# Two graph layers on one core: the q and k projections taken for two pairs of batch elements at once, with a new written order of work

## The chip, the core and the metric

The kernel runs on one core of one Trainium2 chip. The metric is the device time in microseconds of one execution of the whole kernel, from the inputs in HBM to the output in HBM. For the kernel before the change it is the median of three runs. One further execution was taken by the hardware profiler; the views below come from it.

## The reference

128 batch elements of 128 nodes with 512 features go through two layers; all values are float32. The first layer is masked attention with 8 heads of 64 features, the second a graph attention whose scores are sums of two numbers per node. Each has a residual and a normalisation without weights.

```python
# x: (128, 128, 512), adj: (128, 128) of 0 and 1
q = (x @ Wq + bq).reshape(b, n, H, HD)      # H = 8, HD = 64; k and v alike
scores = einsum('bqhd,bkhd->bhqk', q, k) / sqrt(HD) + (1 - adj) * -1e9
attn = softmax(scores)
x = layernorm(x + einsum('bhqk,bkhd->bqhd', attn, v).reshape(b, n, d) @ Wo + bo)

h = x @ W;  s1 = h @ a1;  s2 = h @ a2
e = leaky_relu(s1[:, :, None] + s2[:, None, :], 0.2) * adj
x = layernorm(x + elu(softmax(e) @ h + beta * h))
```

## The kernel before

The batch is worked off in 64 pairs `g` of two elements `b0` and `b1`. A pair is needed because the five products with a 512 x 512 weight (`q`, `k`, `v`, `w` for Wo, `h` for the second layer's W) are each done by seven block products instead of eight: the weight is cut into 2 x 2 blocks of 256 x 256, and x into two halves of its features for each of the two elements. `weight_sum` prepares the sums of weight blocks once. `block_sum` (L245) makes four sums of x blocks per pair on GpSimd, and the seven calls `product(name, g, n)` (L278) with n = 1 to 7 accumulate in PSUM, in `main` (n = 1, 2, 3, 5, 6) and `side` (n = 7, 4). `take_part` (L344) copies a partial sum out to SBUF, on ScalarE for q, k, v and h, on VectorE for w, and `add_block` (L360, VectorE) adds a further part to what was copied. So an accumulator is read while it is still going to grow, and the next product into it waits for that read.

For v, w and h the x side is the stationary operand and the weight streams past it, 256 columns in one matmul. For q and k it is the other way round, because their output has to have features in partitions: a weight block of 128 x 128 is stationary and x streams past it, one element's 128 nodes, so 128 columns in one matmul. A float32 matmul of the source appears in the trace as two matmul instructions. A product of q or k is thus 8 instructions of 128 columns, a product of v, w or h 4 instructions of 256 columns.

The rest of a pair's way, by function: `turn_x` (L237) transposes x blocks on VectorE after `fetch_blocks` has loaded them; `scores` (L370) and `mask`, `row_max`, `exps`, `normalise` make the attention weights; `attn_write` (L422) stores them in a DRAM scratch and `attn_read` (L427) fetches them back with rows and columns of blocks exchanged, as four DMAs; `turn_attn` (L444, VectorE) finishes the transposition; `attend` (L454) multiplies with v. Then come `w`, a normalisation (`norm_c`), the second layer's edge weights, which also take a way through DRAM, `aggregate` (L642), `h` and the final normalisation (`norm_f`) and `store`. `fetch_x` loads x once more for the residual.

Nothing is scheduled by the compiler. Each function call is given a place, in microseconds, by `at(place, fn, ...)`; the calls are sorted by place and issued in that order, each on its own engine's queue, and semaphores keep the data dependencies. The places are the result of a planner that was run beforehand with a cost for each call; only their order reaches the chip. `rows(g)` gives the places of a pair relative to `g * STEP`, with `STEP = 36.678`; `other` replaces them for the first and last pairs, and `last_rows` holds the order of the last two. Several pairs are under way at once: q and k of a pair are multiplied in the step before its scores, h about 2.5 steps after them. The places of the way through DRAM, for example, are these:

```python
            (12.283, exps, b1, 0), (12.823, attn_write, b0), (16.179, exps, b1, 1),
...
            (21.248, normalise, b1, 3), (21.546, attn_read, b0), (21.948, turn_attn, b0, 0),
            (22.433, attn_write, b1), (23.511, take_part, "v", g, 5, 1, 1),
            (24.964, product, "v", g, 3), (26.507, turn_attn, b0, 1),
            (27.155, add_block, "v", g, 7, 1, 1), (27.181, attn_read, b1),
            (30.486, product, "v", g, 4), (31.193, take_part, "v", g, 3, 0, 1),
            (31.929, turn_attn, b1, 0), (32.334, turn_attn, b1, 1),
            (32.982, add_block, "v", g, 4, 1, 0), (36.883, attend, b1), (38.699, attend, b0),
```

Nearly all DMAs are issued by SyncE (SP), in order; a DMA whose data or buffer isn't ready holds up those behind it. Before the first product, `keep_busy(15, "early")` runs 15 matmuls on an identity (L136). At the end, the last pair does w and h by plain products (`plain`, `end_product`, L671), in halves of 256 columns for h, and `end_store` (L710) writes halves of rows.

## Time and profile before

| | before |
|---|---|
| median of 3 runs | 2378.44 us (2378.03 to 2378.46) |
| profiled execution, its own time | 2378.15 us |
| its span, first to last instruction | 2376.4 us |
| mean granted TensorE clock | 0.998 |
| busy: TensorE / VectorE / ScalarE / GpSimd | 99% / 83% / 67% / 36% of the span |
| DMA | 269.83 MB, mean 114 GB/s |

The span is about 1.8 us shorter than the execution's time. "Busy" counts overlapping matmuls once. In the profile PE is TensorE's matmul side and PEld its weight loads, DVE is VectorE, ACT is ScalarE, POOL is GpSimd, and a "q" behind an engine's name is its queue of DMA issues. PEclk is the TensorE clock that was granted, as a share of full speed.

### The profile page before, as it was taken

The page shows a single profiled execution, that of the slowest core. Times are in us where ns is not written, and L with a number is a line of the kernel's source. Part 1 is how long each engine was busy: PE and PEld are TensorE (multiplying, and loading weights), DVE is VectorE, ACT ScalarE, POOL GpSimd, SP SyncE. Part 2 cuts the span into 40 slices and gives each one's busy share as a digit, 9 for nine tenths or more (in the row PEclk, how much of TensorE's full clock was granted, in tenths as well). Part 3 has the DMA queues.
Part 4 walks back from the last instruction along what each step waited for, and adds up shares of the span by engine and source line. Part 5 has one row for each costly group of instructions (what it writes and reads, how often), then busy time and mean ns, then how long its engine had stood idle before and what let it go on. Part 6 is the DMA issues. An engine that isn't in the chain of part 4 may idle for free.

```text
span 2376.4 us, 50868 instructions
## 1 busy us (share of the span) xinstructions
PE 2354.4 (99%) x17703; PEld 2177.5 (92%) x17703; DVE 1961.7 (83%) x4390; ACT 1591.1 (67%) x5763; POOL 865.5 (36%) x1044
## 2 busy tenths in 40 slices
PE   8999999999999999999999999999999999999998
PEld 8998999999999999999999999999999999999996
DVE  7788788888888888888888888888888888888887
ACT  4675666766766667667666676676666766766665
POOL 6243333433433333334334333343343333433422
PEclk9999999999999999999999999999999999999999
DMA  6333334334343343343443433424434334344432
GB/s 192 108 100 112 116 101 125 107 105 134 92 120 119 107 118 108 108 128 92 121 122 103 119 108 111 126 92 121 123 103 119 107 112 125 92 120 122 116 115 74
DMA packets 256121, 269.83 MB, mean 114 GB/s; under 512 B 57372, under 2 KB 204840, under 8 KB 255480
## 3 DMA queue, kind: packets, MB, share of 16 engines
q1 hardware_dynamic: 254992, 265.45, 37.8%
q8 instruction: 140, 2.29, 0.4%
q14 instruction: 117, 0.96, 0.1%
q0 software_dynamic: 304, 0.85, 0.1%
q10 hardware_dynamic: 568, 0.27, 0.0%
HBM read 157.62 MB, written 108.85 MB: 112 GB/s over the span
## 4 chain that ended last, share of the span: by engine, by line
PE 96%; DMA 1%; DVE 1%; ACT 1%; issue 0%; SPq 0%; POOLq 0%; POOL 0%; DVEq 0%; ACTq 0%
PE pq L307 12%; PE pk L307 12%; PE pv L301 12%; PE ph L301 11%; PE pw L301 11%; PE eq L307 9%; PE psc L379 5%; PE po L454 5%; PE pz L642 5%; PE eh L301 5%; PE ew L301 4%; PE ev L301 4%; DMA xblk<-in_x_dram 1%; DMA wq_sb<-in_L_gnn_Wq_dram 0%; ACT s L401 0%
## 5 line engine op out<-in xcount | busy, mean ns | idle before, releaser
L435 POOL TENSOR_TENSOR x<-x,bo_b_in 128x512 f32<-128x512 f32 x128 | 163.6, 1279 | 863.3 <-DMA x<-in_x_dram 863.3
L401 ACT ACTIVATE s<-s,nmax 128x128 f32<-128x128 f32 x1024 | 396.9, 396 | 61.4 <-DVE nmax L395 61.3
L415 ACT ACTIVATE sb<-s,rinv 128x128 f32<-128x128 f32 x1024 | 325.3, 392 | 0.0
L355 ACT ACTIVATE kT<-pk,bias_c 128x128 f32<-128x128 f32 x512 | 160.2, 364 | 202.2 <-PE pk L307 143.2
L355 ACT ACTIVATE qT<-pq,bias_c 128x128 f32<-128x128 f32 x512 | 160.6, 368 | 157.6 <-PE pq L307 157.6
L505 DVE SCALAR_TENSOR_TENSOR ya<-w,wa_row 128x512 f32<-128x512 f32 x256 | 223.9, 875 | 4.4
L401 ACT ACTIVATION_READ_ACCUMULATOR s<-s,nmax 128x1 f32 x1024 | 199.2, 195 | 0.0
L466 ACT ACTIVATE oT<-po,bias_c 128x128 f32<-128x128 f32 x512 | 139.5, 382 | 80.5 <-PE po L454 80.5
L352 DVE TENSOR_TENSOR w<-pw,x 128x256 f32<-128x256 f32 x252 | 106.3, 422 | 97.3 <-PE pw L301 90.8
L444 DVE STREAM_TRANSPOSE attnT<-ab 128x512 f32<-128x512 f32 x256 | 172.7, 694 | 6.8 <-DMA ab<-scr 6.6
L387 DVE SCALAR_TENSOR_TENSOR s<-psc,amask 128x512 f32<-128x512 f32 x256 | 168.6, 680 | 0.7 <-PE psc L379 0.7
L395 DVE TENSOR_REDUCE nmax<-s 128x8 f32<-128x1024 f32 x128 | 156.1, 1220 | 4.3
L349 ACT COPY h<-ph 128x256 f32<-128x256 f32 x252 | 93.8, 372 | 94.1 <-PE ph L301 94.0
L349 ACT COPY v<-pv 128x256 f32<-128x256 f32 x256 | 94.6, 369 | 84.4 <-PE pv L301 59.9
L240 DVE STREAM_TRANSPOSE xT<-xblk 128x512 f32<-128x512 f32 x128 | 139.4, 1108 | 7.9 <-DMA xblk<-in_x_dram 7.9
L657 DVE SCALAR_TENSOR_TENSOR u<-h,x 128x512 f32<-128x512 f32 x126 | 87.1, 692 | 63.8 <-ACT h L349 61.6
L260 POOL TENSOR_TENSOR tx<-xT 128x256 f32<-128x256 f32 x128 | 94.7, 741 | 119.8 <-PE psc L379 97.1
L301 PE MATMUL pv<-wv_sb,xT 128*128 128x256 f32 x512 | 137.5, 392 | 0.0
L307 PE MATMUL pq<-xT,wq_sb 128*128 128x128 f32 x1024 | 135.9, 276 | 1.2 <-DMA wq_sb<-in_L_gnn_Wq_dram 1.2
L307 PE MATMUL pk<-xT,wk_sb 128*128 128x128 f32 x1024 | 134.8, 275 | 0.6 <-DMA wk_sb<-in_L_gnn_Wk_dram 0.4
L307 PEld LDWEIGHTS pq<-xT,wq_sb 128*128 128x128 f32 x1024 | 130.1, 193 | 4.5 <-issue 1.3
L307 PEld LDWEIGHTS pk<-xT,wk_sb 128*128 128x128 f32 x1024 | 129.1, 192 | 4.2 <-DMA wk_sb<-in_L_gnn_Wk_dram 0.6
(677 smaller groups left out, 6352.6 us busy)
## 6 DMA issues: line engine op xcount, KB each, us to landing
scr<-sb SPq DMA_DIRECT2D x128, 512.0 KB
ab<-scr SPq DMA_DIRECT2D x512, 128.0 KB
x<-in_x_dram SPq DMA_DIRECT2D x128, 256.0 KB
xblk<-in_x_dram SPq DMA_DIRECT2D x254, 128.0 KB
out_dram<-u SPq DMA_DIRECT2D x126, 256.0 KB
pb<-s2d SPq DMA_DIRECT2D x62, 128.0 KB
attd<-att SPq DMA_DIRECT2D x62, 128.0 KB
ab<-attd SPq DMA_DIRECT2D x248, 32.0 KB
```

Source lines behind the costliest of these rows:

```text
L301: nc.tensor.matmul(out, b[:, c, :], a[:, c, :], start=first and c == 0, stop=(c == 1), skip_group_check=True,)
L307: nc.tensor.matmul(out[:, m * N : (m + 1) * N], a[:, c, m * P : (m + 1) * P], b[:, c, :], start=first and m == 0 and c == 0, stop=(c == 1) ...
L349: nc.scalar.copy(dst, src)
L355: nc.scalar.activation(dst[:, m, :], src[:, m * N : (m + 1) * N], AF.Identity, bias=BIAS[name][:, 2 * i + m : 2 * i + m + 1],)
L387: nc.vector.scalar_tensor_tensor(s_t[b][:, j * HP : (j + 1) * HP, :], psc[b][j], SCALE, amask.rearrange("p (o n) -> p o n", o=1).broadcast ...
L395: nc.vector.tensor_reduce(nmax[b], s_t[b], AX.X, ALU.max, negate=True)
L401: nc.scalar.activation(s_t[b][:, h, :], s_t[b][:, h, :], AF.Exp, bias=nmax[b][:, h : h + 1], accum_out=rsum[b][:, h : h + 1],)
L415: nc.scalar.mul(sb[b][:, :, h, :], s_t[b][:, h, :].rearrange("p (b c) -> p b c", c=Q), rinv[b][:, h : h + 1],)
L435: nc.gpsimd.tensor_tensor(xr[b], xr[b], later["bo"], ALU.add)
L444: nc.vector.transpose(attnT[b].rearrange("p h (a r) -> p a h r", r=Q)[:, rows], ab[b].rearrange("p a (h c) -> p a h c", c=Q)[:, rows],)
L466: nc.scalar.activation(oT[b][:, c, :], src[:, c, :], AF.Identity, bias=bv_c[:, c : c + 1])
L505: nc.vector.scalar_tensor_tensor(z, y[b], 1.0, wa_row[j], ALU.mult, ALU.mult, accum_out=s12[g][:, i, j : j + 1])
```

## The change

q and k are multiplied once for two pairs. The transposed x of an even and of the following odd pair lie side by side in one tile, `xT_all`, and their block sums in `xs_all`, so that `factor` gives q and k a moving operand of 256 columns; v still takes one pair's 128 as its stationary operand. `product` for q and k is called for even `g` only; its matmuls are half as many and twice as wide. Each of q and k now has three PSUM tiles of its own, for n = 1, for n = 2 and for n = 7, where a pair before had one each and one shared. `take_part` and `add_block` for q and k move twice as many columns per instruction, and `scores` picks its pair out of the common tile. v's SBUF buffers go from two to four; those of xT and its block sums from two to one for each of the two pairs.

The places are new throughout: `STEP = 72.624` is the step of two pairs, and `rows` has a list for even pairs (with q and k) and one for odd pairs (without). The whole order of the first and last pairs is new too. At the start, x blocks of pairs 0 and 1 are loaded first, half by SP's queue and half by ScalarE's; the small loads on GpSimd's queue (`adj`, `bo`, `a1`, `beta`) move behind the first block sums; the matmuls on the identity go from 15 to 20. At the end the last element's row is stored whole, and the other's halves by two queues.

The diff, without most of the lists of numbers:

```diff
--- before.py
+++ after.py
@@ -16,7 +16,7 @@
 EPS = 1e-5
 ALPHA = 0.2
 NEG = 1000000000.0
-STEP = 36.678
+STEP = 72.624
...
     def load_blocks(g):
-        t = grp.tile([P, G, 4, P], F32, tag="xb", name=f"xblk_{g}", bufs=1)
+        if g == 1:
+
+            t = wk2.tile([P, H, N], F32, tag="attnT", name="xblk_1")
+            t = t.rearrange("p (t b) d -> p t b d", t=G)
+        else:
+            t = grp.tile([P, G, 4, P], F32, tag="xb", name=f"xblk_{g}", bufs=1)
         for a in range(4):
-            (nc.scalar if g == 0 and a >= 2 else nc.sync).dma_start(
+            (nc.scalar if g < 2 and a >= 2 else nc.sync).dma_start(
                 out=t[a * Q : (a + 1) * Q].rearrange("r t b d -> r (t b) d"),
                 in_=x[g * G : (g + 1) * G, :, a * P : (a + 1) * P].rearrange(
                     "t (b r) d -> r (t b) d", r=Q
...
-    xblk, xn = {0: load_blocks(0)}, {}
+    xblk, xn = {0: load_blocks(0), 1: load_blocks(1)}, {}
...
-    early = keep_busy(15, "early")
+    early = keep_busy(20, "early")
...
     later = {}
 
     def load_later():
+        nc.gpsimd.dma_start(out=adj_sb, in_=adj)
         later["beta"] = broadcast(cpool, beta, 1, "beta_b")
+        later["bo"] = broadcast(cpool, bo, D, "bo_b")
         for j in range(2):
             a_j = a1[j * D : (j + 1) * D].rearrange("f o -> (f o)")
             later["a", j] = broadcast(wk2, a_j, D, "uf")
-        later["bo"] = broadcast(cpool, bo, D, "bo_b")
 
...
-    xT, right, tx, qT, kT, vb, y, hp, main, side, oT, zT, xr = ({} for _ in range(13))
+    right, tx, qT, kT, vb, y, hp, main, side, oT, zT, xr = ({} for _ in range(12))
     BIAS = {"q": bq_c, "k": bk_c}
     OUT = {"q": qT, "k": kT, "v": vb, "w": y, "h": hp}
 
+
+
+    xT_all = cpool.tile([P, NC, G, 2, N], F32, tag="xT", name="xT")
+    xs_all = cpool.tile([P, 4, 2, 2, N], F32, tag="tx", name="tx")
+
     def turn_x(g, t):
-        if t == 0:
-            xT[g] = grp.tile([P, NC, G * N], F32, tag="xT", name=f"xT_{g}")
         nc.vector.transpose(
-            xT[g][:, :, t * N : (t + 1) * N].rearrange("p m (b r) -> p b m r", r=Q),
+            xT_all[:, :, t, g % 2, :].rearrange("p m (b r) -> p b m r", r=Q),
             xblk[g][:, t].rearrange("p b (c m) -> p b m c", c=Q),
         )
 
+    def x_blocks(slots):
+        s = slice(slots, slots + 1) if isinstance(slots, int) else slice(0, 2)
+        b = [xT_all[:, 2 * h : 2 * h + 2, j, s] for h in range(2) for j in range(G)]
+        t = [xs_all[:, i, :, s] for i in range(4)]
+        b11, b12, b21, b22, t1, t2, t3, t4 = (a.rearrange("p c s n -> p c (s n)") for a in b + t)
+        return b11, b12, b21, b22, (t1, t2, t3, t4)
+
     def block_sum(name, g, n):
 
         if name == "x":
-            b11, b12 = xT[g][:, :2, :N], xT[g][:, :2, N:]
-            b21, b22 = xT[g][:, 2:, :N], xT[g][:, 2:, N:]
+            b11, b12, b21, b22, (t1, t2, t3, t4) = x_blocks(g % 2)
         else:
             src = oT if name == "w" else zT
             b11, b12 = src[g * G][:, :2], src[g * G + 1][:, :2]
             b21, b22 = src[g * G][:, 2:], src[g * G + 1][:, 2:]
-        if (name, g) not in tx:
-            tx[name, g] = grp.tile(
-                [P, 4, 2, N], F32, tag=f"t{name}", name=f"t{name}_{g}", bufs=2 if name == "x" else 1
-            )
-        t1, t2, t3, t4 = (tx[name, g][:, i] for i in range(4))
+            if (name, g) not in tx:
+                tx[name, g] = grp.tile(
+                    [P, 4, 2, N], F32, tag=f"t{name}", name=f"t{name}_{g}", bufs=1
+                )
+            t1, t2, t3, t4 = (tx[name, g][:, i] for i in range(4))
         to, a, b = {1: (t1, b12, b11), 2: (t2, b22, t1), 3: (t3, b22, b12), 4: (t4, b21, t2)}[n]
         nc.gpsimd.tensor_tensor(to, a, b, ALU.subtract)
-        right[name, g] = {1: b11, 2: b21, 3: b22, 4: t4, 5: t1, 6: t2, 7: t3}
-
-    def first_blocks(name, g):
-
+        if name != "x":
+            right[name, g] = {1: b11, 2: b21, 3: b22, 4: t4, 5: t1, 6: t2, 7: t3}
+
+    def factor(name, g, n):
+
+        if name in "qkv":
+            b11, b12, b21, b22, (t1, t2, t3, t4) = x_blocks(g % 2 if name == "v" else None)
+            return {1: b11, 2: b21, 3: b22, 4: t4, 5: t1, 6: t2, 7: t3}[n]
         if (name, g) in right:
-            return right[name, g]
-        if name == "x":
-            return {1: xT[g][:, :2, :N], 2: xT[g][:, 2:, :N]}
+            return right[name, g][n]
+
         src = oT if name == "w" else zT
-        return {1: src[g * G][:, :2], 2: src[g * G][:, 2:]}
+        return {1: src[g * G][:, :2], 2: src[g * G][:, 2:]}[n]
+
+    two = {}
 
     def region(name, g, n):
+
 
         if n in (7, 4):
             return side[name, g]
+        if name in "qk":
+            return (two if n == 2 else main)[name, g]
         return main[name, g][:, 1 if n == 2 else 0]
 
     def product(name, g, n):
-        first = False
-        if n == 1:
-            main[name, g] = ps_mm.tile([P, 2, HF], F32, tag="mm", name=f"p{name}_{g}")
-            first = True
-        if n == 7:
-            if name == "k":
-                side["k", g] = side["qk", g][:, 1]
+
+
+        first = n in (1, 7) or (n == 2 and name in "qk")
+        if first:
+            t = ps_mm.tile([P, 2, HF], F32, tag="mm", name=f"p{n}{name}_{g}")
+            if n == 7:
+                side[name, g] = t if name in "qk" else t[:, 0]
             else:
-                t = ps_mm.tile([P, 2, HF], F32, tag="mm", name=f"e{name}_{g}")
-                side["qk", g] = t
-                side[name, g] = t[:, 0]
-                first = True
-
-
+                (main if n == 1 else two)[name, g] = t
         out = region(name, g, n)
         if n in (1, 2) and name not in left:
             a = W_SB[name][:, 2 * (n - 1) : 2 * n, :HF]
         else:
             a = left[name][n]
-        b = first_blocks(name if name in "wh" else "x", g)[n]
+        b = factor(name, g, n)
         if name in "vwh":
             for c in range(2):
                 nc.tensor.matmul(
-                    out, b[:, c, :], a[:, c, :], start=first and c == 0, stop=(c == 1), skip_group_check=True,
+                    out, b[:, c, :], a[:, c, :], start=first and c == 0, stop=(c == 1),
+                    skip_group_check=True,
                 )
         else:
             for m in range(2):
                 for c in range(2):
                     nc.tensor.matmul(
-                        out[:, m * N : (m + 1) * N], a[:, c, m * P : (m + 1) * P], b[:, c, :],
+                        out[:, m, :], a[:, c, m * P : (m + 1) * P], b[:, c, :],
                         start=first and m == 0 and c == 0, stop=(c == 1),
                         skip_group_check=True,
                     )
@@ -315,14 +333,16 @@
         out = OUT[name]
         if name in "qk":
             if g not in out:
-                out[g] = grp.tile([P, NC, G * N], F32, tag=name, name=f"{name}T_{g}", bufs=1)
-            return out[g][:, 2 * i : 2 * i + 2, j * N : (j + 1) * N]
+                out[g] = grp.tile([P, NC, G, 2, N], F32, tag=name, name=f"{name}T_{g}", bufs=1)
+            return out[g][:, 2 * i : 2 * i + 2, j].rearrange("p m s n -> p m (s n)")
         return whole(name, g * G + j)[:, i * HF : (i + 1) * HF]
 
     def whole(name, b):
         out = OUT[name]
         if b not in out:
-            out[b] = wk2.tile([P, D], F32, tag=name, name=f"{name}_{b}")
+            out[b] = wk2.tile(
+                [P, D], F32, tag=name, name=f"{name}_{b}", bufs=4 if name == "v" else 2
+            )
         return out[b]
 
 
@@ -353,15 +373,13 @@
         else:
             for m in range(2):
                 nc.scalar.activation(
-                    dst[:, m, :], src[:, m * N : (m + 1) * N], AF.Identity,
+                    dst[:, m, :], src[:, m, :], AF.Identity,
                     bias=BIAS[name][:, 2 * i + m : 2 * i + m + 1],
                 )
 
     def add_block(name, g, n, i, j):
 
         src, dst = region(name, g, n), block(name, g, i, j)
-        if name in "qk":
-            src = src.rearrange("p (m n) -> p m n", m=2)
...
-        rows = slice(i * N, (i + 1) * N)
+        qs, ks = (t[g - g % 2][:, :, i, g % 2, :] for t in (qT, kT))
         for m in range(HP):
             for j in range(2):
                 feats = slice(j * HD, (j + 1) * HD)
                 nc.tensor.matmul(
-                    psc[b][j][:, m, :], qT[g][feats, m, rows], kT[g][feats, m, rows],
+                    psc[b][j][:, m, :], qs[feats, m, :], ks[feats, m, :],
                     start=True, stop=True,
                 )
...
     def end_store(b, i):
-        nc.sync.dma_start(out=out[b][:, half(i)], in_=u[b][:, half(i)])
+        if b == 2 * NG - 1:
+            if i == 0:
+                nc.sync.dma_start(out=out[b], in_=u[b])
+            return
+        (nc.scalar if i == 0 else nc.sync).dma_start(
+            out=out[b][:, half(i)], in_=u[b][:, half(i)]
+        )
...
+        if g % 2 == 0:
+            return (
+                (-63.18, fetch_blocks, g), (-56.066, turn_x, g, 0), (-50.12, turn_x, g, 1),
+                (-32.921, block_sum, "x", g, 3), (-31.465, block_sum, "x", g, 1),
+                (-28.542, product, "q", g, 1), (-28.403, take_part, "q", g, 1, 0, 0),
+                (-26.676, product, "k", g, 1), (-26.003, product, "k", g, 2),
...
+                (-16.095, fetch_x, b1), (-13.558, product, "k", g, 6), (-12.431, product, "q", g, 5),
...
+                (26.115, attn_read, b0), (26.457, normalise, b1, 3), (28.151, attn_write, b1),
+                (29.815, take_part, "v", g, 3, 0, 1), (31.844, turn_attn, b0, 0),
...
+                (32.855, attn_read, b1), (34.286, turn_attn, b0, 1), (34.906, turn_attn, b1, 0),
+                (35.094, turn_attn, b1, 1), (35.392, attend, b0), (35.411, attend, b1),
...
+            (-41.301, fetch_blocks, g), (-35.447, turn_x, g, 0), (-33.337, turn_x, g, 1),
+            (-32.76, block_sum, "x", g, 3), (-30.129, block_sum, "x", g, 1),
+            (-24.308, block_sum, "x", g, 2), (-21.661, block_sum, "x", g, 4),
+            (14.048, product, "v", g, 1), (22.008, take_part, "v", g, 1, 0, 0),
+            (23.721, product, "v", g, 7), (26.639, product, "v", g, 6),
...
+            (31.35, fetch_x, b0), (32.03, residual, b0), (32.095, add_block, "v", g, 7, 1, 1),
+            (32.359, product, "v", g, 3), (33.369, product, "v", g, 4),
...
-            at(g * STEP + place, fn, *args)
+            at((g // 2) * STEP + place, fn, *args)
...
-    at(0.583, load_later)
-    at(5.685, load_k_and_v)
...
+    at(-1.534, load_k_and_v)
+    at(4.624, weight_sum, "q", 3, nc.vector)
+    at(5.344, weight_sum, "q", 1, nc.vector)
+    at(6.064, weight_sum, "q", 2, nc.vector)
+    at(7.564, load_later)
+    at(7.564, weight_sum, "k", 3, nc.vector)
+    at(8.284, weight_sum, "q", 4, nc.vector)
+    at(8.864, load_weight, w1_sb, w1)
...
+    at((NG // 2 - 1) * STEP + 1.661, load_again, wq_sb, wo)
+    at((NG // 2 - 1) * STEP + -0.94, load_again, wk_sb, w1)
```

## The prediction

> **What bounds the kernel now.** I read the page first: who is busy, and which chain ended last.
>
> ```profile
> span 2376.4 us, 50868 instructions
> PE 2354.4 (99%) x17703; PEld 2177.5 (92%) x17703; DVE 1961.7 (83%) x4390; ACT 1591.1 (67%) x5763; POOL 865.5 (36%) x1044
> ...
> PE 96%; DMA 1%; DVE 1%; ACT 1%; issue 0%; SPq 0%; POOLq 0%; POOL 0%; DVEq 0%; ACTq 0%
> PE pq L307 12%; PE pk L307 12%; PE pv L301 12%; PE ph L301 11%; PE pw L301 11%; PE eq L307 9%; PE psc L379 5%; PE po L454 5%; PE pz L642 5%; PE eh L301 5%; PE ew L301 4%; PE ev L301 4%; DMA xblk<-in_x_dram 1%; DMA wq_sb<-in_L_gnn_Wq_dram 0%; ACT s L401 0%
> ```
>
> TensorE is 96% of the chain, and q and k (pq, pk, eq, all L307) a third of it. Busy alone wouldn't prove that it never waits, so next the windows of a middle stretch, and the chain inside it:
>
> ```profile
> 1000.00:1036.70 36.70, 36.70 (x278) 34.10 (x277) 30.62 (x70) 24.85 (x90) 13.45 (x17) 1.00 0.36 113
> 1036.70:1073.40 36.70, 36.70 (x278) 34.09 (x278) 30.63 (x69) 24.84 (x90) 13.45 (x17) 1.00 0.38 112
> ```
> ```profile
> 1012.79 1.73 PE ph L301 x8
> 1014.52 0.89 PE pk L307 x8
> 1015.41 1.79 PE pq L307 x16
> ```
>
> PE is busy 36.70 of 36.70 us at full clock, and the chain there is PE without a break: the middle is as long as its matmuls. Between the first score matmuls of one pair and the next lie 36.50 us in 55 of 63 intervals. The trace names about 15 us of waits of PE, nearly all in the first 260 us and at the end. The chain also has the price that matters: 16 matmuls of 128 columns take 1.79 us, 8 of 256 take 1.73. Start to start in the trace that is 111.7 and 215.9 ns.
>
> **The change part by part.**
>
> *q and k.* Per pair 14 products of 8 instructions go, 112; over 64 pairs 7168 x 111.7 = 800.4 us. 3584 of 256 columns come. None exists for q and k yet; the nearest row is a product of v, w or h, also with a new weight block for each matmul: 3584 x 215.9 = 773.6 us. Saved: 26.8 us, 0.84 per two pairs, all on the path.
> A rule speaks against part of it. By the Trainium skill, "TensorE: Matmul & The Clock Gate", section "Back-to-back issue gap", a warm matmul costs its columns at 2.4 GHz plus a fixed 2.5 ns. The trace agrees for 256 columns if float32 streams them twice (213.3 + 2.5 = 215.8). For 128 it gives 109.2, and merging two would save one 2.5: 9.0 us over 3584 merges. The trace has 109 ns only for the gap after the first 128-column matmul behind a wide one, then 111.7 on and on: I read it as weight loads that can't keep ahead of short matmuls. I take the trace's 26.8 and keep 9 as the low end.
>
> *Evictions.* These rows bear on them:
>
> ```profile
> L387 DVE SCALAR_TENSOR_TENSOR s<-psc,amask 128x512 f32<-128x512 f32 x256 | 168.6, 680 | 0.7 <-PE psc L379 0.7
> ...
> L355 ACT ACTIVATE kT<-pk,bias_c 128x128 f32<-128x128 f32 x512 | 160.2, 364 | 202.2 <-PE pk L307 143.2 <-DVE kT L365 53.2 <-PE psc L379 5.7
> ...
> L349 ACT COPY v<-pv 128x256 f32<-128x256 f32 x256 | 94.6, 369 | 84.4 <-PE pv L301 59.9 <-DVE v L365 24.6
> ...
> L365 DVE TENSOR_TENSOR kT<-eq,kT 128x256 f32<-128x256 f32 x128 | 54.2, 423 | 30.0 <-PE eq L307 22.7 <-ACT kT L355 0.4
> ```
>
> 1024 activations of 128 columns (321 us busy) become 512 of 256: by the copy row 369 ns each, 189 us. 384 additions of 256 columns at 0.42 become 192 of 512, by the mask row 0.68, bounded by 0.42 and 0.84: 131 us for 161. ACT and DVE get lighter, which buys nothing as PE hides both; a single eviction gets up to 0.3 us slower, covered because the products between two uses of an accumulator double too. Should that cover go, 8 dependent reuses x 0.3 x 32 is 77 us at the very worst.
>
> *Block sums, transposes, scores, DMA bytes* are the same in number and size, but for single-buffered xT: the new order puts the next `turn_x` behind the last v product that reads its half (16.56 against 12.93; 22.50 against 19.88). PSUM: 17 tiles per pair before, 34 per two pairs after, and 8 banks. Six for q and k instead of three leave less for others for a while; I price it at 0, as the bank of n = 2 is freed by one addition, and a gain is excluded.
>
> *Start.* The first product waits for `wq_sb`, and the clock there is half:
>
> ```profile
> 6.73:10.14 3.41, 1.61 (x14) 1.35 (x12) 0.70 (x1) 0.17 (x1) 2.47 (x4) 1.00 0.90 344
> 10.15:13.55 3.40, 3.27 (x15) 3.30 (x16) 2.98 (x4) 0.63 (x2) 0.38 (x1) 0.50 1.00 398
> ```
> ```profile
> 10.28 2.05 PE L307 MATMUL pq<-xT,wq_sb 128*128 128x128 f32 x8 [1.24 <-DMA wq_sb<-in_L_gnn_Wq_dram]
> ```
>
> The 0.5 MB of pair 0's blocks landed at some 255 GB/s, so pair 1's put wq back by 2.0 us; the 0.63 MB that GpSimd's queue moved before 10 us, now later, give some back. ScalarE's queue has two more block DMAs (0.9 us) ahead of the three bias loads; their transpose, which PE ran at 8.84 ahead of the first product, may be 1 us later and still be in time. Four DMA issues (2.9 us on POOL's queue) now lie behind block sums, before those of pair 1 that are due 3.6 us later. First product at 11.5 instead of 10.3: +1.2 (between 0 and +3). The clock: ten more identity matmul instructions add about 1.1 us to the 1.6 busy in the window before 10.14. Keeping full speed for the first products would save up to 1.7; a later start could lose as much. I take 0.
> By the places, from the first q product to the last pair's first scores there are 2302.3 us before (63 steps less 8.4) and 2281.9 after (31.5 steps less 5.8): filling costs +2.6, since both pairs' q and k come ahead of any score.
>
> *End.* From the start of the last product to the end were 9.0 us:
>
> ```profile
> 2367.39 1.03 PE L671 MATMUL plh<-wk_sb,zT 128*128 128x256 f32 x4
> ...
> 2372.42 0.60 ACT L705 ACTIVATE u<-u,nmr,rstdf_('f',63)_25767 128x256 f32<-128x256 f32 x1 [0.16 <-DVE nmr L714]
> ```
>
> In the new order the second element's two halves come last together, with the first element's sums behind them. From that product's start: 2.4 to its exponential; then on DVE two maxima (0.7), three sums (1.3), four statistics (1.7), aggregates and eps (0.7), POOL's power and hops (0.7), shift and norm (0.8), issue and landing (1.8), closing (1.1): 11.2, so +2.2. The product itself starts some 0.5 earlier after the last scores by the places. The store issued by ACT right behind its own norm, instead of SP's fourth in a row (0.45 apart), is in the 11.2. `load_again` moves from 4 to 33 us ahead of the last scores, when q and k are done: no cost. Together +1.7 (0 to +5).
>
> Sum against the profiled execution's own time: 2378.15 - 26.8 + 1.2 + 2.6 + 1.7 = 2356.85. The median of the runs lies 0.3 above that execution, so 2357.1.
>
> **The rivals.**
>
> *1. A wait in every double step, so slower.* The weights' way through DRAM: in the trace, for b1, the write is issued at 1019.67, the four reads at 1023.48, landed at 1027.92 (8.25 us), and `turn_attn` ran at 1028.78. Its places lay 9.5 us apart; for b1 of even pairs they are now 6.75 (28.151 to 34.906), and SP issues `fetch_x`, `fetch_blocks` and `fetch_x` (1 MB) between write and reads. If reads land 1.5 late, DVE stands, and behind it stand additions, `turn_x` and the next masks; PE waits in `attend` for b1. Against it: `attend` also has its place only as an order, and summing PE's work since the last attend (34 products x 0.863, 1.79, 3.9) puts it 1 us later than its place. It begins to hurt beyond about 1 us and eats the gain at 0.68 us per double step (21.3 / 31). At 1.5 us: 2357 + 46 = 2403. Chance 6%; a smaller wait of some 0.3 us (2366), 12%.
>
> *2. Only the fixed cost is saved.* If a merge saves only the page's 2.5 ns, 9.0 is gained and 5.5 lost at both ends: 2374.9, no change. For it: nothing but the rule. Against it: v, w and h products already run at 215.9. 4%.
>
> *3. Start and end go worse,* the first product at 14 with half clock, filling stalls for 5, tail +5: 2357 + 11 = 2368. 5%.
>
> That q and k aren't 256 wide is excluded by the diff.
>
> **How the numbers follow.** The main case, PE still gapless, has 73%: 2357, own range 2349 to 2364. The range of all runs from 2348 (stalls of the first 260 us gone too) to 2370. What a measurement of this kernel can tell from no change is about 0.2%, 4.8 us: faster means below 2373.7. Main case, rival 3 and most small waits are faster (0.90), rival 2 and a few waits the same (0.04), the large wait slower (0.06).
>
> **What would show it.** Right: pq and pk with half as many instructions at the spacing of pv; PE busy for the whole of a middle window; 72.15 us from one even pair's scores to the next's; the first pq near 11.5; the last plh 11 us ahead of the end. Wrong: PE waiting on `attnT` (DVE) or on an eviction once per double step, a DVE wait for `ab` above 1 us, or a spacing of q's matmuls other than 216 ns.

## The result, and the profile after

The changed kernel took 2368.1 us (median of 6 runs, 2365.8 to 2371.9) beside 2378.1 us of the kernel before (6 runs on the same chip, 2377.7 to 2378.5). The ratio is 0.996 (95% interval 0.995 to 0.997): 10.0 us faster, where 21.3 had been forecast. The predicted 2357.1 us was 11 us too low; the range of all cases (2348 to 2370) holds the time, the main case's own range (2349 to 2364) does not. The profiled execution took 2367.0 us, its span 2365.3.

The head of the page and the chain that ended last, of the kernel after:

```profile
span 2365.3 us, 42947 instructions
PE 2332.2 (99%) x14129; PEld 2045.5 (86%) x14129; DVE 1923.8 (81%) x4198; ACT 1494.1 (63%) x5251; POOL 874.8 (37%) x1044
...
PE 86%; DMA 6%; DVE 3%; SPq 3%; issue 1%; ACT 1%; DVEq 0%; ACTq 0%; POOLq 0%; POOL 0%
```

TensorE has 3574 instructions fewer (3584 less for q and k, ten more at the start) and is still "99% busy", but it no longer is 96% of the chain: DMA, VectorE and SP's queue hold 12% between them. The share of busy time alone would have hidden the whole story.

The groups of instructions (busy, mean ns of one, then the idle time of the engine just before them and what ended it):

```profile
L375 ACT ACTIVATE kT<-p1k,bias_c 128x256 f32<-128x256 f32 x256 | 106.2, 466 | 182.9 <-PE p1k L325 182.9
...
L462 DVE STREAM_TRANSPOSE attnT<-ab 128x512 f32<-128x512 f32 x256 | 169.7, 691 | 34.2 <-DMA ab<-scr 34.2
...
L472 PE MATMUL po<-attnT,v 128*64 128x128 f32 x2048 | 132.3, 277 | 10.1 <-DVE attnT L462 9.9
```

The same transposes in the kernel before:

```profile
L444 DVE STREAM_TRANSPOSE attnT<-ab 128x512 f32<-128x512 f32 x256 | 172.7, 694 | 6.8 <-DMA ab<-scr 6.6
```

VectorE stood 34.2 us waiting for the attention weights to come back from DRAM (6.6 before), and TensorE's matmuls waited 9.9 us for VectorE's transpose of them, a wait that the kernel before doesn't show.

A double step is the time of one even and one odd pair, taken from first score matmul to first score matmul. Its two halves, as windows, of the kernel after (PE, PEld, DVE, ACT, POOL busy, the granted clock, the DMA share and GB/s). The first runs from the odd pair's scores to the even pair's, the second from the even pair's to the odd pair's:

```profile
1063.32:1100.27 36.95, 36.95 (x227) 32.68 (x225) 32.54 (x71) 24.09 (x85) 15.69 (x19) 1.00 0.38 111
1100.27:1136.33 36.06, 35.44 (x219) 31.04 (x217) 27.26 (x60) 22.69 (x82) 11.23 (x13) 1.00 0.41 114
```

The first is full of matmuls, and is 36.95 us in all 27 double steps. The second has a hole; it varied from 35.23 to 36.60 us, mean 35.77. 36.95 + 35.22 is 72.17, the step that had been forecast (72.15), so what the wait cost lies in the second half: 27 x (35.77 - 35.22) = 14.8 us.

What happens there: SP's queue, and then the end of the same wait on VectorE and TensorE, in the kernel after:

```profile
397.06 0.34 SPq L440 DMA_DIRECT2D scr<-sb  x1
397.50 0.37 SPq L96 DMA_DIRECT2D x<-in_x_dram  x1
397.96 2.27 SPq L86 DMA_DIRECT2D xblk<-in_x_dram  x4
400.33 0.40 SPq L96 DMA_DIRECT2D x<-in_x_dram  x1
400.82 1.80 SPq L445 DMA_DIRECT2D ab<-scr  x4
```
```profile
408.25 1.30 DVE L462 STREAM_TRANSPOSE attnT<-ab 128x512 f32<-128x512 f32 x2 [1.95 <-DMA ab<-scr]
...
409.61 1.09 PE L472 MATMUL po<-attnT,v 128*64 128x128 f32 x16 [1.15 <-DVE attnT L462]
```

The even pair's second batch writes its weights (`scr<-sb`), six loads of x (1 MB) follow, and only then the four reads. The last read landed at 408.13, 11.07 us after the write was issued; the same way took 8.25 us in the step of the kernel before that the prediction used. There two stores (512 KB) stood between write and reads, and the loads of x came behind the reads:

```profile
1019.67 0.34 SPq L422 DMA_DIRECT2D scr<-sb  x1
1020.07 1.98 SPq L726 DMA_DIRECT2D out_dram<-u  x2
1022.10 1.03 SPq L548 DMA_DIRECT2D s2d<-s2x  x2
1023.48 1.76 SPq L427 DMA_DIRECT2D ab<-scr  x4
...
1025.76 1.91 SPq L81 DMA_DIRECT2D xblk<-in_x_dram  x4
```

Over 26 of the 27 double steps of the trace, the write is always issued 23.02 us after the even pair's first score matmul. What the double step lost is then the landing time less a constant: lost = (last landing after those scores) - 32.71 us, from 0.01 us at a landing of 32.72 to 1.38 at 34.09, correlation 1.00. So TensorE's order forgives 9.69 us from write to landing; the median in the kernel after was 10.13.

By stretches of the profiled execution, against the same stretches of the kernel before (to pair 4's scores; the 54 pairs to pair 58's scores; from there to the end). The forecast column splits the prediction's sum by the double steps whose q and k fall into each stretch, at 0.84 us: first product 1.2 and filling 2.6 less three of them; 27; the tail's 1.7 less two.

| stretch | before, us | forecast | after | rows of x behind the reads (below) |
|---|---|---|---|---|
| to pair 4's scores | 153.99 | +1.3 | +1.7 | +0.7 |
| 54 pairs | 1975.36 | -22.7 | -12.0 | -26.8 |
| to the end | 247.02 | 0.0 | -0.8 | -0.9 |
| span | 2376.4 | -21.4 | -11.1 | -27.0 |

Start and end came out within 0.8 us of the forecast. The middle lost 10.7 us against it: 14.8 us of wait, less some 4.3 us that two early pairs of the kernel before had lost to waits of their own.

### The profile page after: what moved, and what is told of

Read it like the earlier page. It is cut to its first block, busy times and chain, and to the rows that moved or that the text cites. A ratio compares the mean times of both kernels' runs of the same rounds, so it can differ in the third digit from the quotient of the medians.

```text
span 2365.3 us, 42947 instructions
## 1 busy us (share of the span) xinstructions
PE 2332.2 (99%) x14129; PEld 2045.5 (86%) x14129; DVE 1923.8 (81%) x4198; ACT 1494.1 (63%) x5251; POOL 874.8 (37%) x1044
## 4 chain that ended last, share of the span: by engine, by line
PE 86%; DMA 6%; DVE 3%; SPq 3%; issue 1%; ACT 1%; DVEq 0%; ACTq 0%; POOLq 0%; POOL 0%
PE p1w L318 12%; PE p1q L325 9%; PE p1k L325 9%; PE p1v L318 9%; PE p1h L318 8%; PE psc L397 5%; PE pz L660 5%; PE p7q L325 5%; PE p7k L325 5%; DMA ab<-scr 5%; PE p7w L318 4%; PE po L472 4%; PE p7v L318 4%; PE p7h L318 3%; PE p2q L325 2%; PE p2k L325 2%
## 5 line engine op out<-in xcount | busy, mean ns | idle before, releaser
L375 ACT ACTIVATE kT<-p1k,bias_c 128x256 f32<-128x256 f32 x256 | 106.2, 466 | 182.9 <-PE p1k L325 182.9
L372 DVE TENSOR_TENSOR w<-p1w,x 128x256 f32<-128x256 f32 x252 | 105.9, 420 | 140.9 <-PE p1w L318 140.6
L462 DVE STREAM_TRANSPOSE attnT<-ab 128x512 f32<-128x512 f32 x256 | 169.7, 691 | 34.2 <-DMA ab<-scr 34.2
L369 ACT COPY h<-p1h 128x256 f32<-128x256 f32 x252 | 94.5, 375 | 157.8 <-PE p1h L318 151.8
L472 PEld LDWEIGHTS po<-attnT,v 128*64 128x64 f32 x2048 | 109.8, 137 | 38.2 <-DVE attnT L462 15.9
L472 PE MATMUL po<-attnT,v 128*64 128x128 f32 x2048 | 132.3, 277 | 10.1 <-DVE attnT L462 9.9
L660 PEld LDWEIGHTS pz<-attT,x 128*128 128x128 f32 x1024 | 130.5, 193 | 9.8 <-issue 4.9
L369 ACT COPY v<-p1v 128x256 f32<-128x256 f32 x256 | 91.7, 371 | 70.2 <-PE p1v L318 66.1
L660 PE MATMUL pz<-attT,x 128*128 128x128 f32 x1024 | 131.5, 277 | 4.1 <-DVE attT L600 2.7
L318 PE MATMUL p1v<-wv_sb,xT 128*128 128x256 f32 x512 | 133.9, 385 | 0.0
L318 PE MATMUL p1w<-wo_sb,oT 128*128 128x256 f32 x504 | 132.5, 385 | 0.0
```

Source lines behind the costliest of these rows:

```text
L318: nc.tensor.matmul(out, b[:, c, :], a[:, c, :], start=first and c == 0, stop=(c == 1), skip_group_check=True,)
L369: nc.scalar.copy(dst, src)
L462: nc.vector.transpose(attnT[b].rearrange("p h (a r) -> p a h r", r=Q)[:, rows], ab[b].rearrange("p a (h c) -> p a h c", c=Q)[:, rows],)
L472: nc.tensor.matmul(po[b][j * HD : (j + 1) * HD, m, :], vb[b][:, h * HD : (h + 1) * HD], attnT[b][:, j * HP + m, :], start=True, stop=True,)
L660: nc.tensor.matmul(pz[b][:, c, :], x1[b][:, c * P : (c + 1) * P], attT[g][:, i, :], start=True, stop=True,)
```

## The experiments

**The six loads moved out of the way.** The kernel after, steady odd pairs:

```
-            (-41.301, fetch_blocks, g), (-35.447, turn_x, g, 0), ...
+            (-45.6, fetch_blocks, g), (-35.447, turn_x, g, 0), ...
-            (29.459, fetch_x, b1), ... (30.188, residual, b1),
+            (32.9, fetch_x, b1), ... (33.2, residual, b1),
-            (31.35, fetch_x, b0), (32.03, residual, b0),
+            (32.95, fetch_x, b0), (33.3, residual, b0),
```

> The kernel after, with the six loads of x (1 MB) of the steady double steps moved in the written order: the four block loads to just ahead of the attention write of the even pair's second batch, the two row loads (and the two residual additions that use them) to behind its attention reads; nothing is added or left out. Theory A (the reads stand on SP's queue behind 1 MB of x and land some 3 us late, which TensorE waits out in the weighted sum over v of the even pairs): write to landing falls from about 10 to 11 us to 8.5 or less, VectorE's idle time before the turn of the attention weights falls from 34 us to under 10, TensorE's wait for it from 9.9 us to under 2, and the time from 2368.1 to 2353 to 2358 us (12 of the 15.2 us that the 27 double steps lost, less what the next wait takes). Rival B (the chain itself, from the write to the turn, is too long for the new order whatever stands between): the landing moves by under 1 us and the time stays within 2365 to 2371. Rival C (what was lost lies at the start and the end): no change either, 2366 to 2370.

Measured: 2353.3 us (2350.6 to 2355.1), ratio to before 0.9896 (0.9881 to 0.991). Write to landing 8.0 us (median), the 54 pairs 1948.85 us. Theory A held; rivals B and C, which forecast no change, fell. The edit also moves the two residual additions on GpSimd. That it is the loads is read from the relation above (lost time against landing); the additions were not moved alone.

**Only the two row loads moved,** with the blocks left between write and reads:

```
-            (29.459, fetch_x, b1), ... (30.188, residual, b1),
+            (32.9, fetch_x, b1), ... (33.2, residual, b1),
-            (31.35, fetch_x, b0), (32.03, residual, b0),
+            (32.95, fetch_x, b0), (33.3, residual, b0),
```

> The kernel after, with the two row loads of x (and their residual additions) behind the attention reads, and the four block loads left between write and reads. Theory A: what stands ahead of the reads is halved (512 KB instead of 1 MB), so part of the wait goes: reads land 1 to 2 us earlier, time 2357 to 2363 us, between the kernel after and the one with all six loads moved. Rival B or C: 2365 to 2371, no change.

Measured: 2352.2 us (2351.2 to 2353.8), ratio 0.9894 (0.9878 to 0.9911). Not half of the gain, as I had expected, but all of it. SP's queue and the same two halves of a double step:

```profile
394.29 0.34 SPq L440 DMA_DIRECT2D scr<-sb  x1
394.73 2.28 SPq L86 DMA_DIRECT2D xblk<-in_x_dram  x4
397.36 1.73 SPq L445 DMA_DIRECT2D ab<-scr  x4
399.19 0.85 SPq L96 DMA_DIRECT2D x<-in_x_dram  x2
```
```profile
1056.00:1092.94 36.94, 36.94 (x226) 32.65 (x224) 32.18 (x69) 24.25 (x85) 15.82 (x19) 1.00 0.38 112
1092.94:1128.16 35.22, 35.22 (x218) 31.05 (x216) 27.25 (x63) 22.25 (x81) 10.85 (x13) 1.00 0.41 116
```

The write itself lands 3.04 us after its issue (median), and the reads have to wait for that; SP issues the four block loads inside this time, and the reads follow 3.10 us after the write. With the two row loads as well they followed at 3.80 and then took 6.3 us to land instead of 5.2. Landing is at 8.27 us (median), 1.4 us inside what TensorE forgives, so halving the bytes was enough. The hole is gone and the chain is 96% TensorE again:

```profile
PE 96%; DVE 1%; DMA 1%; ACT 1%; SPq 0%; issue 0%; ACTq 0%; POOLq 0%; POOL 0%; DVEq 0%
```

**The same bytes by another queue.** The kernel after in its own order, with the row loads issued by GpSimd:

```
-        nc.sync.dma_start(out=t, in_=x[b])
+        q = nc.gpsimd if (b // G) % 2 and 5 < b // G < 58 else nc.sync
+        q.dma_start(out=t, in_=x[b])
```

> The kernel after, in its own order, with the two row loads of x of the odd pairs (6 to 57) issued by GpSimd's queue instead of SP's: the same bytes at the same places, in another queue. Theory A1 (the reads of the attention weights are late because they stand behind these bytes in SP's own queue): write to landing falls from 10.1 us (median of after) to under 9, TensorE's wait for the transposed weights goes, time 2351 to 2356 us. Theory A2 (the bytes are in the way whatever queue they come by, since the 16 DMA engines are shared): landing stays at 9.5 or more, 2361 to 2369. Either could lose some: GpSimd issues two DMAs more per double step, which its block sums then stand behind.

Measured: 2360.3 us (2359.3 to 2361.5), ratio 0.9924 (0.9911 to 0.9936): between the two ranges, just below that of A2. The landing lies in A2's range: 9.85 us (median) after the write, 10.06 at the most. But the edit did more than change the queue: the loads also went out at other moments. SP's queue and GpSimd's:

```profile
396.51 0.34 SPq L441 DMA_DIRECT2D scr<-sb  x1
396.95 2.45 SPq L86 DMA_DIRECT2D xblk<-in_x_dram  x4
400.78 1.26 SPq L446 DMA_DIRECT2D ab<-scr  x3
```
```profile
396.28 0.58 POOL L97 DMA_DIRECT2D x<-in_x_dram  x1
...
403.18 0.58 POOL L97 DMA_DIRECT2D x<-in_x_dram  x1
```

The first row load (256 KB) went out 0.23 us ahead of the write, where SP had issued it 0.45 us behind it; the second went out some 6.6 us after the write, behind the reads. The write now took 4.25 us to land instead of 2.98, and the reads could be issued only at 4.29. So bytes of another queue were in the way of write and reads, but queue and moment changed together, and A1 and A2 are not cleanly told apart. By the Trainium skill ("DMA: Bandwidth & Descriptors", "Issuing engines are not separate DMA queues") DMAs of all issuing engines run interleaved on the same 16 engines; this run agrees in so far as the first row load, issued ahead of the write, landed some 0.4 us behind it: the two were under way at once. What went with the shorter time was a narrower spread of the landings: 26 double steps lost 0.14 us on average instead of 0.53, by the same constant of 32.71.

**The wait made in the old order.** The kernel before, steady pairs:

```
-            (-44.347, fetch_blocks, g), (-35.5, turn_x, g, 0), ...
+            (-46.4, fetch_blocks, g), (-35.5, turn_x, g, 0), ...
```

> The kernel before, with the four block loads of x of the steady pairs moved from behind the attention reads of the second batch to between its write and its reads: makes the suspected queueing in the old order, and changes nothing else. Theory A: the reads land 1.5 to 2.5 us later (8.25 to about 10 us after the write was issued); the old order had 0.86 us of slack on VectorE and 2.0 us on TensorE, so a wait of 0 to 0.6 us in each of 54 pairs: 2378 to 2410, likeliest 2390, and VectorE's idle time before the turn over 34 us instead of 6.6. Rival B: landing within 0.5 us of before, 2377 to 2380 us.

Measured: 2450.4 us (2449.7 to 2452.3), ratio 1.0306 (1.0291 to 1.0321): 73 us slower, where 0 to 32 was expected. The group of the transposes in this kernel:

```profile
L444 DVE STREAM_TRANSPOSE attnT<-ab 128x512 f32<-128x512 f32 x256 | 173.1, 695 | 82.5 <-DMA ab<-scr 82.5
```

The landing moved to 10.26 us (median; 7.70 and 8.00 in the even and odd pairs of before): with the stores, 1 MB stands ahead of the reads here too. VectorE's slack of 0.86 us was read at a landing of 8.25 us, so it should stand some 1.1 us a pair; its wait grew by 75.9 us over 59 waits, 1.29 each, and the pairs got 1.33 us longer (2047.04 against 1975.36 us over 54). My mistake was to let TensorE's 2.0 us of slack at the weighted sum stand behind it. TensorE waited there for only 3.0 us in all; it waited 26.2 for ScalarE's eviction of v and 8.7 for VectorE's q instead (these named waits are 38 of the 72 us that the pairs lost). ScalarE in its turn waited 117.4 us for a maximum that VectorE makes behind that transpose (`emax`), where it had waited 7.4 before, and 129.5 instead of 61.3 for another (`nmax`). So the delay reached TensorE by the work queued behind the standing VectorE, and taken over the pairs none of it was absorbed.

**The width alone undone,** in the kernel after and in the one with the rows behind the reads; every 256-column matmul of q and k as two:

```
-                    nc.tensor.matmul(out[:, m, :], a[...], b[:, c, :], ...)
+                    for s in range(2):
+                        cols = slice(s * N, (s + 1) * N)
+                        nc.tensor.matmul(out[:, m, cols], a[...], b[:, c, cols], ...)
```

> The kernel after, with every 256-column matmul of q and k issued as two of 128 columns, all else as it is: undoes the width alone. Theory A (the width is worth what was forecast, 7168 x 111.7 ns - 3584 x 215.9 ns = 26.8 us, and is eaten elsewhere): 2368.1 + 26.8 = 2395 us (2391 to 2398), all of it in the half of the double step from the odd pair's scores to the even pair's, 36.95 to about 37.8 us; the other half keeps its wait. Rival D (a wide matmul saves only its own fixed 2.5 ns or so, and the 10 us came from something else): 2368 to 2378.

> The kernel with the row loads behind the reads (2352.2 us), with every 256-column matmul of q and k issued as two of 128: the price of the width in an order without the wait. Theory (width is worth 26.8 us and the run with the narrow matmuls in the kernel after came out 5.6 us higher because its wait and its start differed): 2379 us (2377 to 2381), odd to even half 37.79 us, even to odd half 35.22 to 35.3, and equal to the kernel before, so that all else of the change is worth nothing together. Rival (issuing them in two costs more than the width alone, by the second weights): 2384 us.

Measured in the kernel after: 2400.5 us (2400.0 to 2401.9), 32.4 above it and above my range. The half from odd to even scores went from 36.95 to 37.79 us, 22.7 us over 27; the other half's wait grew by 4.8 us (landing at 10.46 us), and the start of this execution was 4.7 us later, of which the width explains 2.5 (three double steps). In its trace the first product came 0.8 us later and the clock was at half from 11.88 to 15.29 us, which the start of the kernel after doesn't have.

Measured without the wait: 2380.3 us (21 runs, 2378.8 to 2384.3), 28.1 above 2352.2. The 54 pairs went from 1948.55 to 1971.43 us: 0.847 us per double step, where 0.84 had been forecast. The even to odd half stayed at 35.23:

```profile
999.66:1037.45 37.79, 37.79 (x338) 36.41 (x337) 31.93 (x70) 24.27 (x85) 15.70 (x20) 1.00 0.37 110
1037.45:1072.67 35.22, 35.22 (x218) 31.12 (x217) 27.21 (x62) 22.25 (x81) 10.86 (x13) 1.00 0.42 116
```

Beside the kernel before the ratio is 1.0014 (1.0008 to 1.0021): with the wait cured, all of the change but the width costs some 3 us.

**The other two parts undone** (on the kernel with the rows behind the reads): the second pair's first blocks, and the last stores, by SP alone.

```
-            (nc.scalar if g < 2 and a >= 2 else nc.sync).dma_start(
+            (nc.scalar if g == 0 and a >= 2 else nc.sync).dma_start(
-        (nc.scalar if i == 0 else nc.sync).dma_start(
+        nc.sync.dma_start(
```

> The kernel with the row loads behind the reads (2352.2 us), with the two queue parts of the change undone: the second pair's first blocks of x all by SP, and the last stores all by SP. If they are worth what the profile suggests: SP issues two more loads of 0.5 us at the start ahead of the weights, and the last store is issued some 0.4 us later: 2353.2 us (2352 to 2355). If the loads on ScalarE's queue only held back the biases: 2351 to 2352. Start and end are told apart by the first q product (10.2) and by the time from the last product's start to the end.

Measured: 2353.4 us (2350.8 to 2353.8), which overlaps the 2351.2 to 2353.8 of the kernel it was made from. The median is where it was expected and the profiled execution's first product came at 10.65 instead of 10.19, but a gain of 1 us from the two queues is not shown.

**The clock at the start.** 15 identity matmuls, as before, and then 26, instead of 20:

```
-    early = keep_busy(20, "early")
+    early = keep_busy(15, "early")
```

> The kernel with the row loads behind the reads (2352.2 us), with 15 identity matmuls at the start as in the kernel before instead of 20. Theory (the clock at the start is granted by how long TensorE stood idle before the first product): the gap ahead of the bias transpose grows from 1.9 to about 2.6 us, the granted clock falls to half for some 3.4 us after the first product, which costs 1.7 us: first scores at 38.0 instead of 36.3, 2353.9 us. Rival (the clock was full for another reason, as the first products came later in the pattern of loads): clock full, 2352 us.

Measured: 2354.8 us (2353.1 to 2358.7). The profiled execution is the slowest of the four; in it the first scores came at 42.1 instead of 36.3, more than the 38.0 expected. TensorE's first products, with 15:

```profile
10.19 0.20 PE L145 MATMUL early<-ident,bias_rows 12*128 12x12 f32 x1 [3.66 <-DMA bias_rows<-in_L_gnn_bv_dram]
10.32 2.81 PE L325 MATMUL p1q<-xT,wq_sb 128*128 128x256 f32 x8
12.92 2.80 PE L325 MATMUL p7q<-tx,s_q 128*128 128x256 f32 x8
15.56 1.89 PE L325 MATMUL p1k<-xT,wk_sb 128*128 128x256 f32 x8
...
35.03 3.61 PE L325 MATMUL p7k<-tx,wk_sb 128*128 128x256 f32 x8 [2.04 <-DVE kT L383]
```

and with 20:

```profile
10.06 0.20 PE L145 MATMUL early<-ident,bias_rows 12*128 12x12 f32 x1 [1.66 <-DMA bias_rows<-in_L_gnn_bv_dram]
10.19 1.99 PE L325 MATMUL p1q<-xT,wq_sb 128*128 128x256 f32 x8
12.02 1.89 PE L325 MATMUL p7q<-tx,s_q 128*128 128x256 f32 x8
```

The start to start of the first two products is 2.60 and 2.64 us where it is 1.83 and 1.72: half clock (0.50 granted from 12 to 14 us), which costs 1.7 us. Later TensorE waits 2.04 us for VectorE, and the product behind that wait again takes 3.4 us instead of 1.7. Together that is 5.4 of the 5.8 us.

But 15 or 20 doesn't decide it alone. In the profiled executions with 15 (the kernel before, the blocks between in the old order, this one) the clock fell to half at the first products in all three; with 20 it did in three of eight (both kernels with narrow matmuls, and the one below with the output rows moved, from 11.20 to 14.61 us). With 26 it did in none of three. Which part of a wait counts is worked out in the last section. The later wait for VectorE (0.5 to 2.0 us) is found in three of the four executions of the new order whose first products ran at half clock, and in none of the eight others; that the slow start causes it isn't shown.

```
-    early = keep_busy(20, "early")
+    early = keep_busy(26, "early")
```

> The kernel with the row loads behind the reads (2352.2 us), with 26 identity matmuls at the start instead of 20, so that TensorE stands idle for under 1 us ahead of the bias transpose. Theory (the start has two outcomes: an idle time of up to 2.0 us leaves the granted clock full, one of 2.3 or more halves it, and the same kernel falls now on one side and now on the other, which makes the spread of its runs): clock full, first scores at 36.3, 2351.5 us (2350.5 to 2352.5), runs within 2 us of each other. Rival (the spread comes from the DMA landings in the filling): 2352 us with the spread as before, 2351 to 2355.

Measured: 2352.9 us (2351.1 to 2355.1). Clock full and first scores at 36.2, as expected; but the runs are no closer together than before. The spread is not settled by the clock at the start, and its cause stays open.

**The tail.** On the kernel with the rows behind the reads, the last pair's output rows in the room of `xblk`; then, with 26 identity matmuls, VectorE's last operations in another order as well (and the first element's row, not the second's, stored whole):

```
         if b not in u:
-            u[b] = wk2.tile([P, D], F32, tag="uf", name=f"u_{b}")
+            if "last" not in u:
+                u["last"] = grp.tile([P, G, 4, P], F32, tag="xb", name="u_last", bufs=1)
+            u[b] = u["last"][:, b % G].rearrange("p b d -> p (b d)")
```

> The kernel with the row loads behind the reads (2352.2 us), with the output rows of the last pair in the room of the blocks of x, which nothing uses any more, instead of in the two buffers that the stores of the pair before still read. Theory: VectorE's idle 4.0 us ahead of the last pair's first maximum (for the DMA out of u) goes, its maxima, sums and statistics of the first element run while TensorE still makes the second's products, and from the last product's start to the end it takes 9 us instead of 11.95: 2349.5 us (2348.5 to 2350.5). Rival (the end is bound by ScalarE's exponentials or by the last element's own chain, and the idle time lies beside them): 2351.5 to 2352.5.

Measured: 2352.8 us (2351.7 to 2355.3): no gain beyond the spread. The wait for the store is gone, and from the last product's start to the end the profiled execution took 11.06 us instead of 11.96; VectorE still did two of its four maxima, and all its statistics, behind ScalarE's last exponential. The idle 4.0 us lay mostly beside something else, as the rival said.

```
-            (93.407, end_max, b0, 1), (93.767, end_max, b1, 0),
-            (94.127, end_sum, b1, 0), (94.547, end_max, b1, 1), (94.907, end_max, b0, 0), ...
+            (93.407, end_max, b0, 1), (93.45, end_sum, b0, 1), (93.5, end_stats, b0, 1),
+            (93.6, end_max, b0, 0), (93.7, end_sum, b0, 0), (93.8, end_stats, b0, 0), ...
```

> The kernel with 26 identity matmuls, with the last pair's output rows in the room of the blocks of x and VectorE's last operations put in order: the first element's maxima, sums, statistics, norm and store as soon as its products are there, and only the second element's last half behind the last product. Theory (the tail was long since VectorE did both elements' sums and statistics behind the last product): from the last product's start to the end 8.5 us instead of 11.1, 2349 us (2348 to 2350). Rival (ScalarE's exponentials behind the norm of the pair before, 1.5 us, set the end): 2351 us.

Measured: 2349.4 us (2348.3 to 2351.7), ratio 0.9884 (0.987 to 0.9897). The tail is 8.72 us, 8.5 expected. The new order was not run without the moved rows.

**Fillers in the last gap.**

```
+        if g == NG - 3 and not any(k in pz for k in (2 * g, 2 * g + 1)) and "fill" not in pl:
+            pl["fill"] = keep_busy(10, "fill")
```

> The kernel with the end in order (the second of these four), with 10 identity matmuls (2.2 us) put into TensorE's idle 3.1 us ahead of the third last pair's aggregation. Theory (that idle time halves the granted clock, so that the 16 aggregation matmuls behind it take 3.4 us instead of 1.8): clock full there, 1.0 to 1.6 us less: 2347.5 us. Rival (the bank that the fillers take holds back another product, or the aggregation has slack to the end): 2349 to 2351 us, as without.

Measured: 2348.6 us (2347.0 to 2349.2), ratio 0.9878 (0.9865 to 0.9892). It is the fastest version of all, 28.8 us under before and 19.5 under the kernel after, but its 0.8 us over the one without fillers is inside the spread, and the reason given for it isn't borne out. The aggregation behind the gap, first in the kernel with the rows behind the reads, then in that with the end in order, neither with fillers:

```profile
2300.35 3.42 PE L660 MATMUL pz<-attT,x 128*128 128x128 f32 x16 [2.70 <-DVE attT L600]
```
```profile
2302.80 2.02 PE L660 MATMUL pz<-attT,x 128*128 128x128 f32 x16 [2.71 <-DVE attT L600]
```

The same wait of 2.7 us was followed by half clock in one execution and by full clock in the other. The windows of 3.41 us around them, first and second kernel (the third number from the end is the granted clock):

```profile
2296.45:2299.86 3.41, 1.20 (x6) 0.72 (x4) 3.38 (x10) 3.41 (x15) 0.00 (x0) 1.00 0.59 162
2299.86:2303.27 3.41, 2.92 (x14) 2.95 (x15) 3.27 (x11) 1.89 (x6) 0.00 (x0) 0.50 0.51 183
```
```profile
2298.49:2301.90 3.41, 1.61 (x8) 1.08 (x6) 3.38 (x9) 3.41 (x16) 0.00 (x0) 1.00 0.60 170
2301.90:2305.31 3.41, 2.51 (x19) 2.46 (x20) 3.34 (x10) 2.75 (x8) 0.00 (x0) 1.00 0.51 170
```

How these windows are laid, and why the two waits differ, is told in the last section.

## Why the prediction was wrong, point by point

- **The width: right.** 0.84 us per double step forecast, 0.847 measured without the wait. Over the 112 wide matmuls of a double step that is 7.6 ns saved by each, and in the kernel after the wide matmuls of q and k follow each other at 215.9 ns (mean of the middle). The rule weighed in the prediction (the Trainium skill, "TensorE: Matmul & The Clock Gate", "Back-to-back issue gap") would have given 2.5 ns each, by the estimate made there 9.0 us in all. What the prediction left out is that the section gives it for an isolated matmul and says that in a stream with weight loads both set the spacing. The measurement decides for the trace's 111.7 and 215.9 ns.
- **"The main case, PE still gapless", 73%: the step that failed.** The sum has no term for a wait on the attention weights' way through DRAM. Its size was 14.8 us (27 x 0.55 us), and it showed as the prediction had said that being wrong would: TensorE waiting for `attnT` once per double step. Rival 1 named the place, the loads between write and reads, and the mechanism, and it came true in the small form that I gave 12% (0.3 us, 2366). What spoke against it, that TensorE reaches the weighted sum later than its place, was true but mis-sized: the order forgives 1.44 us more than the 8.25 of before, and the reads were 1.9 us later (median), up to 2.8. I estimated the slack and never the delay, although 1 MB at the 344 to 398 GB/s of the windows that I showed of before is 2.6 to 3.0 us of DMA time.
- **What made up for part of it.** In the kernel before, two of the 54 pairs, between 190 and 267 us, took 4.0 us more than the 36.50 of nearly all others; over the whole middle such losses come to 4.3. Without the wait, the new order lost nothing there (1948.55 us against 27 x 72.17 = 1948.6). The prediction had that only in the low end of its range.
- **Start: near in sum by luck, wrong in its parts.** The first product came at 10.2, not 11.5, and in this execution the clock stayed full, a gain that I had put at 0 (in three of the eight with 20 identity matmuls it didn't). The window that was at half clock before, of the kernel after:

```profile
10.15:13.55 3.40, 3.40 (x16) 3.00 (x17) 3.33 (x4) 1.01 (x3) 3.40 (x5) 1.00 1.02 424
```

  Those are 1.3 and 1.7 us better than forecast. Since pair 4's scores still came 0.4 us later than by the sum, the filling (with the other waits of the start) cost some 3.4 us more than its 2.6.
- **End: near in sum,** 0.8 us below it. From the last product's start to the end 11.95 us, 11.2 forecast. The working missed that the last pair's rows use the buffers that the stores of the pair before still read:

```profile
2353.30 1.03 PE L689 MATMUL plh<-wk_sb,zT 128*128 128x256 f32 x4
...
2355.03 0.42 DVE L700 SCALAR_TENSOR_TENSOR u<-plh,x 128x256 f32<-128x256 f32 x1 [4.01 <-DMA out_dram<-u]
```

  That, with VectorE's order, is worth 3.2 us of tail (11.96 to 8.72).
- **Evictions: mis-sized, at no cost.** An activation of 256 columns with bias took 466 ns, not the copy row's 369. TensorE hid it, as assumed.

## What to carry to other kernels

When loads move in a hand-written order, look on the issuing queue for a round trip through DRAM (a write, then reads of it) and work out two numbers: how late the consumer can be fed, and how many bytes now run ahead of the reads. Loads that fit into the time in which the write lands anyway cost no measurable time here (2352.2 us with 512 KB of them, 2353.3 without); the next 512 KB cost more than half of the change's gain, and moving those two loads gave it back. Slack of the last consumer isn't slack of the chain: an in-order engine that stands for a DMA passes the delay on to all that is queued behind it.

## What the runs showed of the hardware that was not expected

- A load in another queue got in the way of a write: with 256 KB issued by GpSimd 0.23 us ahead of it, the write landed after 4.25 us instead of 2.98.
- The granted clock went by a fixed grid. In the 11 profiled executions with more than one stretch of half clock, these stretches begin whole multiples of 3.413 us apart, to within 2 ns (with 15 identity matmuls at 11.35, 35.24, 2308.52 and 2349.48 us: 7, 666 and 12 steps). Each lasts 3.41 us, and longer only at the end, where TensorE has nothing left to do.
- What counted was the idle time inside one window of this grid. Cut along their grids, from the first record of the clock on, the 14 executions have 9693 windows. All 47 windows in which TensorE's matmuls left 2.04 us or more idle were followed by half clock in the next one, and none of the 9641 windows with up to 1.74 us was; of the five between (1.80 to 2.01) two were. So what goes with half clock is how much of a wait falls into one window, not its whole length.
- That explains the waits that looked alike. Of the 2.7 us ahead of the aggregation 2.21 us fell into one window in the first of the two kernels shown above, 1.81 and 0.90 into two in the second. The wait of 2.0 us behind VectorE lay whole in one window; of the 2.0 us ahead of the bias transpose in the kernel after no window held more than 1.22 us, and its clock stayed full. Where the grid lies against the kernel changes from one execution to the next. The Trainium skill ("TensorE: Matmul & The Clock Gate", "Part 1: The HAM clock gate") gives an idle window of about 3.4 us as the condition; here 2.04 us idle within a window were enough.
